# Three convolution steps per attention step on the first chunks, and a looser gate between chunks

## The chip, the cores and the metric

The kernel runs on one core of a Trainium2 chip. The metric is the time of one execution on the device in microseconds, as the median of several runs. The engines named below are TensorE (PE, with its weight loads PEld), VectorE (DVE), ScalarE (ACT), GpSimd (POOL) and SyncE (SP), which here does nothing but issue DMAs.

## The reference, cut to what matters

```python
def _qz_ring(phi):
    c = jnp.cos(phi)
    P = jnp.cumprod(c, axis=-1)
    z0 = jnp.prod(c[..., 1:], axis=-1, keepdims=True)
    return jnp.concatenate([z0, P[..., 1:]], axis=-1)
...
# x: [4, 128, 64, 64]
# layer 0
x = x + _L0_conv_ref(_gn(x), w_off, b_off, w_mask, b_mask, weight, bias)   # deformable 3x3
# layer 1, tokens: [4, 4096, 128], 16 heads of 8
t = _to_tokens(x)
...
qkv = _qz_ring(heads + rx_theta)          # heads come from _ln_t(t); q = k = v
scores = jnp.einsum('bhsd,bhtd->bhst', q, q) / np.sqrt(D)
ctx = jnp.einsum('bhst,bhtd->bhsd', jax.nn.softmax(scores, axis=-1), q)
...
# then w_comb, a norm, a small feed-forward part, a norm;
# at the end a mixture of 8 experts of which each token takes 2
```

The deformable convolution samples the normed image at nine shifted places for each position (four corners each, weighted bilinearly and by a mask), and multiplies the nine samples of 128 channels by a 128 x 128 matrix each. Its result, added to the input, is the residual stream; the attention's queries, keys and values are all the same "features", products of cosines of the normed tokens.

## The kernel before, in words

**Tiles and stages.** An image has 4096 positions, cut into 8 chunks of 512; the 16 heads are 4 groups of 4. A chunk of an image goes through three stages before attention can use it.

1. *Samples* (`deform`). A unit is 128 positions x 3 taps. POOL gathers the corners from a table in DRAM (L622, three indirect DMAs a unit), DVE multiplies by the weights (L642) and adds the four corners (L647, L648). For chunks 0 and 1 of the first image PE transposes the samples (L659) and DVE copies them into `sT_first` (L662). For all other chunks DVE transposes blocks (L685), SP writes them to DRAM (`smd`, L697) and reads them back as `sT` (L730).
2. *Convolution* (`convolved`). 9 taps x 2 halves, each a group of four matmuls that the helper `by_columns` issues (L275), into one PSUM bank `conv_ps`; these 18 groups are what is called "the convolution of a chunk" below. Then DVE adds bias and input (L757), PE transposes (L764), and DVE copies the result to `x2` (L766).
3. *Features* (`features`). Norm statistics (L779, L780), the root on POOL (L390), the normed tokens `xt` (L787), cosines (L367 to L383), products (L815 to L821, into `rn`), a copy by POOL for the values (L822, written by SP at L826), four PE transposes (L835, `fT_ps`), and a high and a low part on DVE (`hiT` L837, `loT` L838), which SP writes as keys and queries with eight DMAs (L845, L846).

**Attention** is a list of *runs*; a run is one group of heads, one chunk of queries (`sc`) and a list of steps of 128 keys. A step has four score matmuls (L1249), two exponentials on ACT (L1258) and four context matmuls into the bank `acc` (L1266). The keys and values of a chunk are loaded at L1227 and L1229, the queries of a run at L1237. Because the first image's features appear chunk by chunk, its first 26 runs (the "opening") work on what there is: runs 0 to 3 take chunk 0 alone (four steps each), runs 4 to 11 add chunk 1 (48 steps), runs 12 to 17 chunk 2 (40 steps), runs 18 to 25 chunk 3. Where a run continues an earlier sum, its partial sum `cu` is loaded from DRAM (L1438), added to `acc` by DVE (L1470), and stored again (L1125); a first sum is copied (L1468).

**Order.** The order of PE, DVE, SP and POOL is fixed at build time by a planner, the class `Beside`. It keeps an estimated clock (`now`, one step is 1.82 us) and estimated times at which DVE and POOL come free. Side work is written as generators, which yield what they need (PE time, DVE time, a wait) before each piece. On every attention step `step` (L132) runs, in this order: up to eight pieces without PE work, one piece with PE work (a "fill", such as one convolution group), and again up to eight pieces without. A fill also needs credit, which a step gives and a fill uses up; the credit may be overdrawn by `LATE`. When attention can't go on, `force` runs side work at once. Emits put into `later` (DMAs of SP, gathers of POOL) go out when the estimated clock gets there. ACT's instructions are the exponentials in the order of the steps.

**The gates.** The list `featuring` holds an entry from the moment a chunk's convolution is queued until its features are done (`featuring.clear()`, L851). The convolution of chunk 0 or 1 is queued only when the list is empty (L672), and so is that of every other chunk (L708). `summed` gets an entry for each finished convolution.

Of the kernel before, what the change touches and what calls it, by code (L numbers as in the profile page):

```python
# [61 lines left out]
class Beside:  # L62
# [9 lines left out]
    def __init__(self):  # L72
        self.now = self.credit = self.dve = self.pool = self.bank = 0.0
        self.lock = None
        self.rate = self.RATE
        self.queue = []
        self.deferred = []

# [53 lines left out]
    def step(self, backlog):  # L132

        self.now += self.STEP
        self.flush(self.now)
        self.credit = min(self.credit + self.rate, self.RATE)
        for fills, limit in ((False, min(0.8, backlog)), (True, backlog), (False, backlog)):
            for _ in range(1 if fills else 8):
                job = next(
                    (j for j in self.queue  # L140
                     if (j["need"][0] > 0) == fills and self._fits(j, limit)), None
                )
                if job is None or (fills and self.credit - job["need"][0] < -self.LATE):
                    break
                self._run(job)

# [50 lines left out]
def need(pe=0.0, dve=0.0, lat=0.0, hold=False, after=0.0):  # L197

    return pe, dve, lat, hold, after
# [17 lines left out]
def kernel(  # L219
# [376 lines left out]
    def deform(b, tab, idx, wt, rest):  # L596


        units = [
            (ch, kg, j) for ch in range(NCH) for kg in range(3) for j in range(4 * ch, 4 * ch + 4)  # L600
        ]
        ahead = []
        issued = 0

        def early(n):

            return b == 0 and n < 3 * 12

        def gather(last):

            nonlocal issued
            while issued < len(units) and issued <= last + (4 if early(issued) else 2):
                n = issued
                issued += 1
                _, kg, j = units[n]
                if early(n) and n % 5 > 2:
                    v = spare(f"v{b}_{j}_{kg}")[:, : 12 * C].rearrange("p (k q) -> p k q", k=3)
                else:
                    v = work.tile([P, 3, 4 * C], F32, tag="v", name=f"v{b}_{j}_{kg}", bufs=NV)
                for k in range(3):  # L620
                    kk = 3 * kg + k
                    nc.gpsimd.indirect_dma_start(  # L622
                        out=v[:, k, :], out_offset=None, in_=tab,
                        in_offset=bass.IndirectOffsetOnAxis(ap=idx[:, j, kk : kk + 1], axis=0),
                    )
                ahead.append((v, beside.gathered()))

        sent = 0.0
        moved = []
        gather(-1)  # L630
        for n, (ch, kg, j) in enumerate(units):
            progress[b] = 0.1 + 0.9 * n / len(units)
            if b == 0 and n == 36:
                yield need(dve=5.0)
                settle()
            while not ahead:
                yield need(lat=0.5)
            v, landed = ahead.pop(0)
            v4 = v.rearrange("p k (q c) -> p (k q) c", c=C)
            w12 = wt[:, j, 3 * kg : 3 * kg + 3, :].rearrange("p k q -> p (k q)")  # L640
            yield need(dve=ve(1536), after=landed)
            nc.vector.tensor_tensor(v4, v4, w12[:, :, None].to_broadcast([P, 12, C]), ALU.mult)  # L642
            if moved:
                yield need(pe=0.01, dve=ve(384))
                moved.pop()()
            yield need(dve=ve(768) + ve(384))
            nc.vector.tensor_tensor(v[:, :, : 2 * C], v[:, :, : 2 * C], v[:, :, 2 * C :], ALU.add)  # L647
            nc.vector.tensor_tensor(v[:, :, :C], v[:, :, :C], v[:, :, C : 2 * C], ALU.add)  # L648
            if b == 0 and ch < 2:


                if n % 12 == 0:
                    while len(summed) < ch:
                        yield need(lat=0.5)
                    sT = big.tile([P, KK, CH], F32, tag="xs", name=f"sT_first{ch}")
                yield need(pe=tr(3), lat=FREE, hold=True)
                pt = misc(f"sT_ps{j}_{kg}")
                for k in range(3):
                    nc.tensor.transpose(pt[:, P * k : P * (k + 1)], v[:, k, :C], ident)  # L659

                def move(sT=sT, kg=kg, i=j % 4, pt=pt):
                    nc.vector.tensor_copy(  # L662
                        sT[:, 3 * kg : 3 * kg + 3, P * i : P * (i + 1)],
                        pt[:, : 3 * P].rearrange("p (k c) -> p k c", c=P),
                    )

                moved.append(move)
                beside.later(beside.now + 0.8, lambda n=n: gather(n))
                if n % 12 == 11:
                    yield need(pe=0.01, dve=ve(384))  # L670
                    moved.pop()()
                    while featuring:  # L672
                        yield need(lat=0.5)
                    featuring.append(True)
                    beside.add("prepare", convolved(b, ch, sT), 0.5, True)
                    if ch == 0:
                        yield from rest
                continue

            yield need(dve=ve(384))  # L680
            if j % 4 == 0:
                beside.flush(sent)
                tr9 = work.tile([P, 4, 4, 4, 32], F32, tag="st", name=f"tr{b}_{ch}_{kg}", bufs=NST)
            for k in range(3):
                nc.vector.transpose(  # L685
                    out=tr9[:, k, :, j % 4, :],
                    in_=v[:, k, :C].rearrange("p (c i) -> p c i", i=32),
                )
            beside.later(beside.dve, lambda n=n: gather(n))
            if j % 4 < 3:  # L690
                continue
            while kg == 0 and len(featuring) > 1:
                yield need(lat=1.0)

            def put(ch=ch, kg=kg, tr9=tr9):
                for o in range(4):
                    nc.sync.dma_start(  # L697
                        out=smd[ch % 2][:, 3 * kg : 3 * kg + 3, :, o].rearrange(
                            "i k c n -> i (k c) n"
                        ),  # L700
                        in_=tr9[32 * o : 32 * (o + 1), :3].rearrange("p k c j t -> p (k c) (j t)"),
                    )

            sent = beside.dve
            beside.later(sent, put)
            if kg == 2:

                while featuring:  # L708
                    yield need(lat=1.0)
                featuring.append(True)  # L710
                beside.later(
                    beside.dve + 0.1,
                    lambda ch=ch: beside.add("prepare", convolved(b, ch), 0.5, True),
                )
        while featuring:
            yield need(lat=1.0)
# [75 lines left out]
    def features(b, ch, x2, mean, rstd):  # L792
# [55 lines left out]
        beside.later(beside.dve - ve(512), lambda: put(0, hi))  # L848
        beside.later(beside.dve, lambda: put(1, lo))
        prepared[b, ch] = beside.dve + 9.0  # L850
        featuring.clear()  # L851

    def prepare(b):
        xs = big.tile([P, KK, CH], F32, tag="xs", name=f"xc{b}")
# [279 lines left out]
    def turn(es, run, t):  # L1134
        b, g, sc = runs[run][:3]
        kt = t % 4
        st = work.tile([P, 4, 4, P], F32, tag="st", name=f"st{run}_{t}", bufs=NST)
        beside.dve = max(beside.dve, beside.now + 0.9)
        for pr in range(2):
            nc.vector.transpose(  # L1140
                out=st[:, :, 2 * pr : 2 * pr + 2, :].rearrange("p o h (q j) -> p o (h q) j", j=32),
                in_=es[pr].rearrange("p h (q o i) -> p o (h q) i", o=4, i=32),
            )
            beside.dve += ve(1024)

        turned = etd[g][sc % 2][kt].rearrange("(o i) r x -> r i o x", i=32)

        def put():
            for r in range(4):
                nc.sync.dma_start(  # L1150
                    out=turned[r], in_=st[32 * r : 32 * (r + 1)].rearrange("p o h x -> p o (h x)")
                )
            turning.discard((g, sc % 2, kt))

        turning.add((g, sc % 2, kt))
        beside.later(beside.dve, put)
# [237 lines left out]
    with tc.manual_schedule(engines={PE, DVE, SP, POOL}):  # L1394
# [6 lines left out]
        while n < len(steps):  # L1401
# [15 lines left out]
            for m in (n, n + 1):  # L1417
                if m < issued and steps[m] in gives:
                    gives.remove(steps[m])
                    turn(es[m - n], *steps[m])  # L1420
            if streaming:
                backlog = 1.5
            else:
                backlog = 0.4 if at >= len(ts) - 3 else 3.2
# [125 lines left out]
```

## Time and profile before

| | |
|---|---|
| five runs, us | 7711.37, 7739.1, 7725.41, 7725.62, 7700.86 |
| median | 7725.41 |
| profiled execution, its own time | 7713.76 |
| its span | 7712.0 |
| busy PE / weight load | 7163.4 (93%) / 2524.6 (33%) |
| busy ACT | 6871.0 (89%) |
| busy DVE | 4480.8 (58%) |
| busy POOL | 1654.6 (21%) |
| exponentials, L1258 | 7400 of 1066 ns, 6867.8 in all |
| context matmuls, L1266 | 29600 of 605 ns, 3963.0 in all |
| score matmuls, L1249 | 14800 of 500 ns (those with a record), 2387.4 in all |

All times are microseconds from the start of the span unless marked ns. Busy times of different engines overlap, so they don't add up to the span. The profile of the first 520 us, in which the first image's opening runs, is where the diff acts: chunk 1 is used first by run 4, chunk 2 by run 12 and chunk 3 by run 18. The first scores of these runs start at 296.04, 405.55 and 492.08; ACT's first exponential of run 4 starts at 296.93 after 71.27 idle, and that of run 12 at 406.15. The features of these chunks reach their transposes (L835) at 264.56, 371.23 and 471.49.

### The profile page before, as it was taken

Reading aid. Unit: us, or ns where it says so; the run is one execution under the profiler, and the core shown is the slowest. Engines: PE = TensorE matmul, PEld = TensorE weight load, DVE = VectorE, ACT = ScalarE, POOL = GpSimd, SP = SyncE. Lnnn points to the kernel's source line nnn. Section 1 sums busy time; section 2 is a strip of 40 time slices with the busy share of each in tenths; the row PEclk is TensorE's granted clock in tenths of the full one; section 3 lists DMA queues with packets and bytes.
Section 4 is the critical chain, followed back from the end, with each engine's and each line's share of the span. In section 5 each row is a group of like instructions: output and inputs, shape, how many; then the busy total and the mean of one; then the engine's idle time right before and its main releaser. Section 6 shows DMA issues by size and latency. Waiting matters only on the chain.

```text
span 7712.0 us, 181988 instructions
## 1 busy us (share of the span) xinstructions
PE 7163.4 (93%) x73736; PEld 2524.6 (33%) x73736; DVE 4480.8 (58%) x8976; ACT 6871.0 (89%) x7441; POOL 1654.6 (21%) x1326
## 2 busy tenths in 40 slices
PE   3589899899999999999999989989999999999997
PEld 2122233223333333333333323333333333333333
DVE  6766356666444767776544676765444545445444
ACT  0579899789999899999999988989999999999995
POOL 5545034443001323422000333431000000000000
PEclk6789999999999999999999999999999999999998
DMA  5677477878557878887766788898665577777762
GB/s 183 204 227 228 131 234 244 285 239 280 161 159 218 264 234 268 277 270 240 209 176 189 240 255 280 286 304 246 188 185 160 151 252 242 246 237 253 240 217 74
DMA packets 922615, 1730.71 MB, mean 224 GB/s; under 512 B 169074, under 2 KB 393356, under 8 KB 871084
## 3 DMA queue, kind: packets, MB, share of 16 engines
q1 hardware_dynamic: 821918, 1412.48, 60.1%
q0 software_dynamic: 92160, 302.06, 12.0%
q8 instruction: 579, 9.49, 0.5%
q10 hardware_dynamic: 7694, 4.52, 0.2%
q14 instruction: 264, 2.16, 0.1%
HBM read 1059.11 MB, written 659.57 MB: 223 GB/s over the span
## 4 chain that ended last, share of the span: by engine, by line
PE 84%; DMA 5%; DVE 4%; issue 3%; ACT 3%; SPq 1%; another core or an unknown queue 0%; POOL 0%; ACTq 0%; POOLq 0%; DVEq 0%
PE acc L1266 41%; PE sc L1249 24%; PE acc L1202 6%; PE conv_ps L275 4%; PE e_ps L275 4%; ACT e L1258 3%; PE f_ps L275 2%; DMA et<-etd 1%; PE om_ps L530 1%; DMA sT<-smd 1%; DMA etd<-st 1%; DVE v L642 1%; PE ao_ps L275 0%; DMA kT<-kTd 0%; DMA qT<-qTd 0%
## 5 line engine op out<-in xcount | busy, mean ns | idle before, releaser
L1258 ACT ACTIVATE e<-sc 128x1024 f32<-128x1024 f32 x7400 | 6867.8, 1066 | 704.4 <-PE sc L1249 425.0
L1266 PE MATMUL acc<-e,qf 128*32 128x512 f32 x29600 | 3963.0, 605 | 23.5 <-DVE cu L1468 13.3
L1249 PE MATMUL sc<-qT,kT 32*128 32x512 f32 x14800 | 2387.4, 500 | 238.6 <-ACT e L1258 142.7
L1249 PEld LDWEIGHTS sc<-qT,kT 32*128 32x128 f32 x14800 | 954.6, 183 | 3635.9 <-ACT e L1258 3055.1
L622 POOL DMA_INDIRECT v<-tab,idx x1152 | 1452.2, 1261 | 1742.3 <-DVE tr L685 1104.6
L1140 DVE STREAM_TRANSPOSE st<-e 128x1024 f32<-128x1024 f32 x792 | 937.6, 1222 | 781.1 <-ACT e L1258 599.6
L1266 PEld LDWEIGHTS acc<-e,qf 128*32 128x32 f32 x29600 | 802.9, 110 | 591.2 <-issue 339.6
L390 POOL TENSOR_TENSOR r<-ln_t,expo 128x4 f32<-128x4 f32 x96 | 112.3, 1170 | 3134.7 <-DVE ln_t L388 3087.5
L642 DVE TENSOR_TENSOR v<-v,wt 128x1536 f32<-128x1536 f32 x384 | 665.9, 1734 | 90.7 <-DMA v<-tab,idx 76.1
L1202 PE MATMUL acc<-et,qf 128*32 128x128 f32 x12672 | 522.3, 281 | 39.5 <-DMA et<-etd 33.4
L1064 DVE TENSOR_TENSOR eo<-e_ps,gt 128x512 f32<-128x512 f32 x256 | 175.1, 686 | 544.4 <-PE e_ps L275 536.8
L1202 PEld LDWEIGHTS acc<-et,qf 128*32 128x32 f32 x12672 | 302.5, 110 | 239.6 <-issue 190.2
L647 DVE TENSOR_TENSOR v<-v 128x768 f32<-128x768 f32 x384 | 367.5, 957 | 9.7
L275 PE MATMUL conv_ps<-sT,wconv_sb 128*32 128x256 f32 x4320 | 352.1, 398 | 16.5 <-DMA sT<-smd 13.8
L1468 DVE COPY cu<-acc 128x512 f32<-128x512 f32 x128 | 88.5, 691 | 385.0 <-PE acc L1266 327.6
L685 DVE STREAM_TRANSPOSE tr<-v 128x128 f32<-128x128 f32 x1080 | 249.4, 282 | 43.6 <-DMA etd<-st 35.1
L648 DVE TENSOR_TENSOR v<-v 128x384 f32<-128x384 f32 x384 | 215.7, 562 | 13.3
L275 PE MATMUL f_ps<-w_sb,h 128*32 128x128 f32 x4096 | 166.5, 281 | 1.3 <-issue 1.2
L390 POOL TENSOR_TENSOR rstd<-lt_t,expo 128x4 f32<-128x4 f32 x32 | 55.7, 1742 | 513.5 <-DVE lt_t L388 504.6
L949 DVE TENSOR_SCALAR h<-h_ps,b_sb 128x512 f32<-128x512 f32 x128 | 94.9, 744 | 102.3 <-PE h_ps L947 91.5
L822 POOL COPY fx<-rn 128x512 f32<-128x512 f32 x32 | 29.6, 925 | 530.3 <-DVE rn L821 348.0
L964 DVE TENSOR_TENSOR a<-a,f_ps 128x512 f32<-128x512 f32 x32 | 22.0, 687 | 199.8 <-PE f_ps L275 199.8
(224 smaller groups left out, 3147.9 us busy)
## 6 DMA issues: line engine op xcount, KB each, us to landing
etd<-st SPq DMA_DIRECT2D x1584, 256.0 KB
et<-etd SPq DMA_DIRECT2D x396, 1024.0 KB
kT<-kTd SPq DMA_DIRECT2D x400, 256.0 KB
smd<-tr SPq DMA_DIRECT2D x360, 192.0 KB
sT<-smd SPq DMA_DIRECT2D x360, 192.0 KB
qf<-fqd SPq DMA_DIRECT2D x400, 144.0 KB
qT<-qTd SPq DMA_DIRECT2D x166, 256.0 KB
atd<-cu SPq DMA_DIRECT2D x128, 256.0 KB
```

Of the source, the lines that this page charges most:

```text
L275: nc.tensor.matmul(dst[c : c + 32], lhsT=lhsT[:, c : c + 32], rhs=rhs, start=start, stop=stop)
L622: nc.gpsimd.indirect_dma_start(out=v[:, k, :], out_offset=None, in_=tab, in_offset=bass.IndirectOffsetOnAxis(ap=idx[:, j, kk : kk + 1], ax ...
L642: nc.vector.tensor_tensor(v4, v4, w12[:, :, None].to_broadcast([P, 12, C]), ALU.mult)
L647: nc.vector.tensor_tensor(v[:, :, : 2 * C], v[:, :, : 2 * C], v[:, :, 2 * C :], ALU.add)
L648: nc.vector.tensor_tensor(v[:, :, :C], v[:, :, :C], v[:, :, C : 2 * C], ALU.add)
L685: nc.vector.transpose(out=tr9[:, k, :, j % 4, :], in_=v[:, k, :C].rearrange("p (c i) -> p c i", i=32),)
L1064: nc.vector.tensor_tensor(ws[hf], pe.rearrange("p (e c) -> p e c", c=C), gt[:, i, 4 * hf : 4 * (hf + 1), None].to_broadcast([P, 4, C]), AL ...
L1140: nc.vector.transpose(out=st[:, :, 2 * pr : 2 * pr + 2, :].rearrange("p o h (q j) -> p o (h q) j", j=32), in_=es[pr].rearrange("p h (q o i ...
L1202: nc.tensor.matmul(acc[32 * h : 32 * (h + 1), P * kt : P * (kt + 1)], lhsT=qf[:, t, QW * h : QW * h + 32], rhs=e[:, :, h, 32 * t : 32 * (t ...
L1249: nc.tensor.matmul(ps[i // 2][:, i % 2, :], lhsT=kT[h : h + 32, P * (t % 4) : P * (t % 4 + 1)], rhs=qT[h : h + 32, :], start=True, stop=True,)
L1258: nc.scalar.activation(e, ps[pr], AF.Exp, scale=1.0 / math.sqrt(HD))
L1266: nc.tensor.matmul(acc[32 * h : 32 * (h + 1), :], lhsT=qf[:, t % 4, QW * h : QW * h + 32], rhs=es[h // 2][:, h % 2, :], start=(t == ts[0]) ...
```

## The change

The diff has two parts.

*Fills.* The planner gets an attribute `fills`, 1 at first. Where it is above 1, `step` runs up to that many pieces with PE work in one step, and the test on the credit is dropped. The main loop sets it to 3 in runs 0 to 11 and to 1 from run 12 on; before the first attention step it has its first value.

*Gates.* The convolution of chunk 0 or 1 is queued without looking at `featuring`. That of a later chunk of the first image waits until the convolutions of all chunks in front are finished (`len(summed) < ch`), and no longer until their features are; the later images keep their gate. At the end of a chunk's features one entry of the list is taken out rather than all.

The line numbers of the changed kernel are one higher than those of the kernel before from L76 on, three higher from L143, one higher from L674, and three higher again from L1421.

```diff
@@ class Beside, __init__
         self.rate = self.RATE
+        self.fills = 1
         self.queue = []
@@ step
         for fills, limit in ((False, min(0.8, backlog)), (True, backlog), (False, backlog)):
-            for _ in range(1 if fills else 8):
+            for _ in range(self.fills if fills else 8):
                 job = next(
                     (j for j in self.queue
                      if (j["need"][0] > 0) == fills and self._fits(j, limit)), None
                 )
-                if job is None or (fills and self.credit - job["need"][0] < -self.LATE):
+                if job is None or (
+                    fills and self.fills == 1 and self.credit - job["need"][0] < -self.LATE
+                ):
                     break
                 self._run(job)
@@ deform, chunks 0 and 1 of the first image
                     moved.pop()()
-                    while featuring:
-                        yield need(lat=0.5)
                     featuring.append(True)
@@ deform, the other chunks
             if kg == 2:
-                while featuring:
+                while len(summed) < ch if b == 0 else featuring:
                     yield need(lat=1.0)
                 featuring.append(True)
@@ features, at the end
         prepared[b, ch] = beside.dve + 9.0
-        featuring.clear()
+        featuring.pop(0)
@@ the main loop, before step is called
                     turn(es[m - n], *steps[m])
+
+            beside.fills = 3 if run < 12 else 1
             if streaming:
```

## The prediction

> **What bounds the kernel now.** I read the page first: ScalarE (ACT) is busy for 89% of the span, TensorE (PE) for 93%, nearly all of it in the attention steps (L1249 scores, L1258 exponential, L1266 context). Its slices show both low only in the first tenth. Then the table by stage of that tenth:
>
> ```profile
> 175.00:226.00 51.00, 38.85 (x301) 13.21 (x305) 34.17 (x47) 30.57 (x32) 41.09 (x32) 0.77 0.73 234
> 226.00:296.00 70.00, 5.52 (x61) 3.30 (x53) 62.73 (x130) 0.00 (x0) 42.50 (x31) 0.55 0.65 196
> 296.00:400.00 104.00, 93.17 (x700) 27.84 (x700) 63.05 (x120) 86.09 (x93) 43.84 (x32) 0.90 0.70 211
> 400.00:520.00 120.00, 96.84 (x748) 28.29 (x744) 75.76 (x137) 88.92 (x96) 58.52 (x45) 0.84 0.80 238
> ```
>
> Columns: stretch, length, busy time (and count) of PE, weight load, DVE, ACT, POOL, then granted clock, DMA share, GB/s. From 226 to 296 ACT does nothing and PE 5.5 of 70 us, while DVE works 62.7 of 70: attention has used up chunk 0 and waits for chunk 1's features. From 296 to 520 DVE is busy 139 of 224 us, so there it has some 85 us to spare. PE's timeline shows the chain inside the hole:
>
> ```profile
> 198.75 1.08 PE L275 MATMUL conv_ps<-sT_first,wconv_sb 128*32 128x256 f32 x8
> ...
> 226.20 3.14 PE L275 MATMUL conv_ps<-sT_first,wconv_sb 128*32 128x256 f32 x44
> 238.79 1.09 PE L764 MATMUL x_ps<-ident,xr 128*128 128x128 f32 x4 [9.45 <-issue]
> 264.56 1.09 PE L835 MATMUL fT_ps<-ident,rn 128*128 128x128 f32 x4 [24.68 <-DVE rn L821]
> 296.04 1.22 PE L1249 MATMUL sc<-qT,kT 32*128 32x512 f32 x6 [30.39 <-DMA kT<-kTd]
> ```
>
> Chunk 1's convolution is spread over 31 us of attention; its result then queues on DVE behind products of chunk 2 (residual add at 237.57), and after the features SP's queue makes the last gap:
>
> ```profile
> 269.31 0.66 SPq L845 DMA_DIRECT2D kTd<-hiT  x1
> ...
> 277.20 6.15 SPq L697 DMA_DIRECT2D smd<-tr  x4
> 283.40 1.10 SPq L721 DMA_DIRECT2D xr<-in_x_dram  x1
> 284.59 2.79 SPq L730 DMA_DIRECT2D sT<-smd  x4
> 287.43 0.43 SPq L1227 DMA_DIRECT2D kT<-kTd  x1
> ```
>
> The keys' load waits 10 us behind chunk 2's smd, xr and sT issues.
>
> **The change, edit by edit.** The order of instructions on each engine, the two kernels side by side, says what the planner makes of it. *The gates* (L672, L708, L851): with these alone the order on every engine is that of before, so they cost and bring 0; no cover is needed, since nothing moves. *Three fills a step*: chunk 1's 72 matmuls go out in six bursts of 12 instead of fours, the first one step earlier; chunk 2's mostly in twelves too; DVE, SP and POOL follow. ACT's order is the same throughout, no instruction is added or removed, and after chunk 6's features all orders are equal again, so whatever is won or lost by then stays. I follow the chain by rows.
>
> 1. *PE.* A step of before with one group is 0.44 (L1249) + 0.57 (L275) + 0.86 (L1266) = 1.87 us in the chain of waits; ACT alone needs 0.92 x 2 = 1.84 (34.97 us for 38). With a burst it is 0.44 + 3 x 0.57 + 0.86 = 3.0: each burst holds ACT up by 1.16 us, some 12 bursts 14 us, behind no cover. The convolution ends at 196.87 + 3.05 (first burst, cold) + 5 x 1.7 + 4 x 0.87 + 4 x 0.44 = 213.7 instead of 229.3.
> 2. *DVE.* The residual add now stands behind cu1 and the tenth block's multiply: 214.3, x2's copy 218.2 (before 242.44). Then copy and statistics 2.7, cu2 0.7, v11 3.3, xt 1.1, cosine and products 12.2, cu3 0.7: rn ends at 238.9 (before 264.4). rstd on POOL (2.5 us) hides behind v11, as its gather queue is empty by 218. A stream transpose and one multiply (2.35) stand before hiT: 241.2, loT to 242.6 (before 269.2). The eight blocks of chunk 2 (28 to 35) that stood ahead, 8 x 3.95 = 31.6 us (1.72 + 0.96 + 0.56 + 0.70), are done later, under ACT's work of runs 4 to 7. Chunk 2's gathers now queue on POOL behind fx (239 to 241); five units x 3.9 us from 241 still keep ahead of DVE, which ends chunk 2 at 272 (before 273.8).
> 3. *SP.* One smd group 2.7, fqd 2.65, eight key and query writes 7.8, to 252.9; the load may go when they have landed, 4.15 us in chunk 0 (164.87 to 169.02), so 257.1. From load to first score it took 5.5 us in chunk 0 and 8.6 in chunk 1: 262.6 to 265.7, and I take 264. Run 4 starts 32 us earlier than 296.04. smd, xr and sT of chunk 2 now come behind the keys, where they have until 286.
> 4. *Runs 4 to 11.* qT5 goes out at 265 behind the next smd and lands in 7.1 as before (301.89): 272, against 309.1. Eight steps at 1.84, six with bursts at 3.0, 21 at 1.84: 344. There cu10's partial sum waits behind chunk 2's key writes on SP (issued 347, landing in 4 to 8.5): 351 to 356. Run 12's exponential follows 12.2 (without the 3.44 us wait for kT) to 15.6 us later: 367, against 406.15. Gain 39.
> 5. *Runs 12 to 18.* 40 steps took 83.4 us (406.15 to 489.5); kept, they end at 450.4. Here the change adds a wait: chunk 3's transposes (L835), which stood 12 steps ahead of that end (471.49), now stand behind the last context matmul. On PE run 18's scores queue behind them; hiT, the eight writes, smd 3.8, xr 0.9, four loads 1.8 and eight sT issues 6.7 then put qT19 at 474, and with the 11.3 us that it took (504.81 to 516.09) run 19 starts at 485.3, against 516.1. Gain 31: eight of the 39 are given back.
> 6. *After.* Same matmuls, nearly the same order; the stall of run 34 (863 to 906) hangs on chunk 7's order, which is equal. 0, with -8 to +8 for the waits between 568 and 604 and from 692 to 700, which can fall either way.
>
> **Rules against the rows.** The first group took 1.08 us where the granted clock was low and 0.64 later; if all six bursts ran at the first, they would end at 196.9 + 6 x 3.24 + 4 x 1.93 + 4 x 0.8 = 227, and the gain would fall by 13.6. [...]
>
> qT19 took 11.3 us in a stretch (484 to 517) with a DMA share of 0.94, against 5.5 for chunk 0's first keys; by the short one the gain is 37, and I take the long one, as the same transfers bunch. [...]
>
> **The sum.** 7713.76 us is the profiled execution (span 7712.0, 1.8 around it); minus 31 is 7683. It lies 11.7 below the median of the five runs (7725.41); against the median that is **7694**.
>
> **Rivals.** *More is kept* (10%): qT19 comes in 5.5 us and the waits at 568 and 692 shrink by 8: 7725 - 45 = 7680. For it: those waits sit in DMA-crowded stretches that come apart. Against: SP's order there is nearly the same. *Given back* (23%): the gain of 32 us at run 4 is real but run 18's new wait and the bursts eat it: cold bursts take 13.6, late features of chunk 3 some 6 more: 31 - 20 = 11, 7714. For it: L835 now has nothing behind which to hide. Against: DVE has 85 us to spare before it. *DVE debt* (7%), the other side: the 31.6 us of blocks moved behind chunk 1's features make chunks 2 and 3 late by as much, so run 19 keeps its date (gain 0), while the bursts' 14 and the exposed 8 stay: 7725 + 22 = 7747. It decides once DVE has no idle time between 296 and 517; the table gives it 85 us. *That it does nothing* holds for the gates; for the fills PE's order rules it out.
>
> **Chances.** My sum, 60%, with its own range of 22 to 42 us of gain, 7683 to 7703. A measurement of this kernel tells some 0.3%, 23 us, from no change. Of the 60, 56 lie beyond that, with the 10 above: 0.66 faster; 4 and the 23: 0.27 same; 0.07 slower. The range takes in the first rival and most of the second: 7668 to 7726.
>
> **What would show it.** In the changed kernel's profile: six rows of L278 with some 24 records between 197 and 214; the residual add (L758) near 214; first scores of run 4 at 262 to 266 and the hole in ACT down from 71 to some 37 us; conv 2 in bursts from some 287; run 12 near 367; L836 of chunk 3 only after run 17's last L1267 and a hole of some 20 us there; run 19 near 485. I am wrong if DVE is busy without a break from 296 to 450, if bursts stay at 1.08 a group, or if the lead at run 12 is not near 39 us.

## The result: 7 us, where 31 were forecast

The changed kernel takes 7721.62 us (median of 24 runs, 7707.44 to 7738.11), the kernel before 7729.03 (44 runs): ratio 0.9993, 95% interval 0.9986 to 1.0000. It is at most a hair faster, well inside the 0.3% that the prediction called no change. Chips differ by more: the kernel before took 7591 to 7760 us on those used below, so only ratios on one chip are compared. Two executions, one of begin40 (13058 us) and one of the kernel before beside deep3 (19932 us), ran at granted clocks of 0.46 and 0.58 where all others had 0.96 to 0.97, and no ratio takes them in.

The changed kernel's table by stage shows the hole filled and opened again later. Columns as in the prediction: stretch, length, busy time and count of PE, weight load, DVE, ACT, POOL, granted clock, DMA share, GB/s.

```profile
175.00:226.00 51.00, 39.95 (x320) 13.94 (x324) 30.34 (x53) 27.05 (x29) 32.42 (x28) 0.78 0.64 211
226.00:296.00 70.00, 29.57 (x168) 8.20 (x160) 64.68 (x121) 24.59 (x27) 42.72 (x30) 0.66 0.78 238
296.00:400.00 104.00, 85.55 (x668) 26.54 (x668) 64.74 (x121) 81.64 (x88) 47.59 (x38) 0.91 0.75 225
400.00:520.00 120.00, 83.88 (x660) 26.10 (x652) 77.99 (x143) 70.03 (x76) 59.08 (x45) 0.80 0.74 219
```

From 226 to 296 ACT now works 24.6 us where it did nothing; from 296 to 520 it works 151.7 instead of 175.0. DVE does the same work as before in each row, within 4 us. ACT's exponentials come in the same order in both kernels, so the first one of each run can be set side by side in the two traces (us):

| first exponential of run | 4 | 6 | 7 | 12 | 14 | 18 | 19 | 26 | 34 | 39 | 46 |
|---|---|---|---|---|---|---|---|---|---|---|---|
| before | 296.93 | 326.70 | 333.99 | 406.15 | 422.71 | 492.97 | 516.98 | 630.00 | 816.48 | 915.64 | 1198.16 |
| changed | 267.10 | 297.29 | 310.50 | 383.42 | 406.30 | 499.42 | 518.88 | 628.14 | 811.50 | 911.32 | 1199.33 |
| difference | -29.8 | -29.4 | -23.5 | -22.7 | -16.4 | +6.5 | +1.9 | -1.9 | -5.0 | -4.3 | +1.2 |

Thirty microseconds are won at run 4, and all are gone at run 18. The later differences, up to 16 us either way after run 50, are those of single executions.

PE's timeline of the changed kernel (start, duration, operation, count, idle time before and what ended it) shows the win and the loss:

```profile
196.04 2.79 PE L278 MATMUL conv_ps<-sT_first,wconv_sb 128*32 128x256 f32 x24
...
199.48 2.05 PE L278 MATMUL conv_ps<-sT_first,wconv_sb 128*32 128x256 f32 x24
...
202.76 1.50 PE L278 MATMUL conv_ps<-sT_first,wconv_sb 128*32 128x256 f32 x24
...
242.81 1.12 PE L836 MATMUL fT_ps<-ident,rn 128*128 128x128 f32 x4 [12.16 <-DVE rn L822]
266.21 1.22 PE L1250 MATMUL sc<-qT,kT 32*128 32x512 f32 x6 [22.28 <-issue]
...
468.17 3.37 PE L1267 MATMUL acc<-e,qf 128*32 128x512 f32 x24
471.48 0.66 PE L836 MATMUL fT_ps<-ident,rn 128*128 128x128 f32 x4
498.53 1.22 PE L1250 MATMUL sc<-qT,kT 32*128 32x512 f32 x6 [26.40 <-DMA kT<-kTd]
```

Chunk 1's convolution goes out in bursts of three groups, its features reach the transposes at 242.81 instead of 264.56, and run 4 follows. Chunk 3's features reach theirs at 471.48, directly behind run 17's last context matmuls. Before, that was at 471.49, with nine steps of attention still to come; that the two dates agree so closely is chance. Attention arrives 17 us earlier (run 17's last exponential ends at 470.4, before at 487.1) and waits. The chunk that it waits for has not moved at all, so the lead turns into a wait for the keys: 26.40 us, where run 18's first scores had 2.62 before:

```profile
492.08 1.22 PE L1249 MATMUL sc<-qT,kT 32*128 32x512 f32 x6 [2.62 <-issue]
```

SP's timeline of the changed kernel (start, duration, line, operation, count) shows the keys of chunk 1, which now go ahead of the last `smd` and of `xr` and `sT`, and then those of chunk 3:

```profile
250.00 1.08 SPq L846 DMA_DIRECT2D kTd<-hiT  x1
...
257.32 0.93 SPq L847 DMA_DIRECT2D qTd<-loT  x1
262.80 0.34 SPq L1228 DMA_DIRECT2D kT<-kTd  x1
...
266.90 4.13 SPq L698 DMA_DIRECT2D smd<-tr  x4
...
474.86 0.55 SPq L846 DMA_DIRECT2D kTd<-hiT  x1
...
482.22 0.69 SPq L847 DMA_DIRECT2D qTd<-loT  x1
486.67 3.83 SPq L698 DMA_DIRECT2D smd<-tr  x4
...
491.21 1.21 SPq L1228 DMA_DIRECT2D kT<-kTd  x1
```

Chunk 1's load goes 4.6 us after the last key write's issue ends. Chunk 3's goes 8.3 after it, behind a `smd` of chunk 4. SP stood idle in front of that `smd` for 3.7 us, until DVE had done chunk 4's last sample, whose gather had come late:

```profile
482.57 1.76 DVE L645 TENSOR_TENSOR v<-v,wt 128x1536 f32<-128x1536 f32 x1 [5.41 <-DMA v<-tab,idx]
```

So a few us of the 26.4 are SP's order and chunk 4's sample; the rest is the date of the features.

That chunk 3 did not move is seen in each of its steps, from the same traces:

| chunk 3 | first and last multiply (L642) | last four sT issues, from | convolution | transposes of its features |
|---|---|---|---|---|
| before | 278.6, 379.2 | 413.4 | 412.3 to 447.0 | 471.49 |
| changed | 284.9, 377.2 | 411.0 | 410.4 to 442.6 | 471.48 |

What held it there is mostly PE's order. Counted in steps of attention (eight records of context matmuls each), its convolution stands behind 72 steps now and stood behind 65 before, and its transposes stand behind 104 and stood behind 95. Seven and nine steps of 1.84 us are 13 and 17 us; attention's lead is 16 to 17 us from run 14 on. In front of the convolution PE has no idle time, now or before, so there the convolution waited for the attention steps ahead of it and not for its samples:

```profile
410.41 0.64 PE L278 MATMUL conv_ps<-sT,wconv_sb 128*32 128x256 f32 x8
```

```profile
412.31 0.64 PE L275 MATMUL conv_ps<-sT,wconv_sb 128*32 128x256 f32 x8
```

The planner sets these places by its own estimate of when the samples are there, so samples can act through the order as well as by themselves.

### The profile page after: what moved, and what is told of

Read it like the earlier page. It is cut to its first block, busy times and chain, and to the rows that moved or that the text cites. A ratio compares the mean times of both kernels' runs of the same rounds, so it can differ in the third digit from the quotient of the medians.

```text
span 7726.7 us, 181999 instructions
## 1 busy us (share of the span) xinstructions
PE 7181.7 (93%) x73736; PEld 2528.5 (33%) x73736; DVE 4481.5 (58%) x8976; ACT 6870.9 (89%) x7441; POOL 1647.3 (21%) x1326
## 4 chain that ended last, share of the span: by engine, by line
PE 82%; DMA 6%; DVE 4%; ACT 3%; SPq 2%; issue 2%; another core or an unknown queue 0%; POOL 0%; ACTq 0%; DVEq 0%; POOLq 0%
PE acc L1267 40%; PE sc L1250 24%; PE acc L1203 5%; PE conv_ps L278 4%; PE e_ps L278 4%; ACT e L1259 3%; PE f_ps L278 2%; DMA et<-etd 1%; DMA sT<-smd 1%; PE om_ps L533 1%; DMA etd<-st 1%; DMA qT<-qTd 1%; DVE v L645 1%; PE ao_ps L278 0%
## 5 line engine op out<-in xcount | busy, mean ns | idle before, releaser
L1267 PE MATMUL acc<-e,qf 128*32 128x512 f32 x29600 | 3971.6, 606 | 32.6 <-DVE cu L1473 18.6
L1065 DVE TENSOR_TENSOR eo<-e_ps,gt 128x512 f32<-128x512 f32 x256 | 175.0, 685 | 549.2 <-PE e_ps L278 539.1
L651 DVE TENSOR_TENSOR v<-v 128x384 f32<-128x384 f32 x384 | 215.8, 562 | 13.3
```

The source lines that it names most:

```text
L1065: nc.vector.tensor_tensor(ws[hf], pe.rearrange("p (e c) -> p e c", c=C), gt[:, i, 4 * hf : 4 * (hf + 1), None].to_broadcast([P, 4, C]), AL ...
L1267: nc.tensor.matmul(acc[32 * h : 32 * (h + 1), :], lhsT=qf[:, t % 4, QW * h : QW * h + 32], rhs=es[h // 2][:, h % 2, :], start=(t == ts[0]) ...
```

## The experiments

Three theories at first. P: the dates at which a chunk's samples are taken (gathers on POOL, products on DVE) set when later runs may start. G: the gain is given back at one place, run 18's key writes. B: the bursts hold ACT up. D, a rival of P later on: DVE's work alone sets the samples' dates. All the kernels compute the same result as before.

For every kernel, the table gives the difference of a run's first exponential from that in gates_only, which has the order of before (negative is earlier; us), and the measured ratio to the kernel before on the same chip with its interval. The kernels in it ran on chips where before took 7591 to 7595 us. Each difference is of two single executions: begin40 and changed_again, which have the same order up to run 38, differ by up to 3 us there (6 once), and so much means nothing.

| kernel | run 4 | 12 | 18 | 26 | 31 | 38 | 39 | 46 | ratio to before |
|---|---|---|---|---|---|---|---|---|---|
| changed_again | -32.1 | -22.1 | +1.2 | -5.3 | -7.1 | -7.1 | -9.0 | -6.1 | 0.9990 (0.9981 to 1.0000) |
| begin40 | -32.5 | -22.0 | +2.3 | -3.3 | -4.3 | -4.4 | -24.3 | -37.3 | 0.9995 (0.9985 to 1.0005) |
| fills4 | -34.3 | +0.3 | -9.9 | -5.5 | -6.3 | -4.2 | -22.5 | -35.5 | 1.0000 (0.9990 to 1.0010) |
| fills18 | -32.7 | -21.2 | -16.6 | -22.9 | -0.2 | +0.8 | +3.5 | -9.6 | 1.0035 (1.0020 to 1.0049) |
| deep3 | -32.2 | -22.2 | -21.2 | -23.6 | -22.5 | -22.6 | -24.3 | -26.4 | 0.9974 (0.9964 to 0.9984) |
| deep3_again | -33.3 | -22.7 | -23.3 | -23.3 | -22.3 | -22.4 | -23.6 | -24.5 | 0.9959 (0.9946 to 0.9972) |
| before_deep3 | +3.9 | +12.8 | +15.1 | +14.7 | +10.0 | +9.8 | -13.1 | -16.3 | 1.0009 (0.9999 to 1.0019) |
| deep8 | -32.9 | -20.8 | +6.7 | +13.8 | +25.8 | +24.8 | -1.4 | -13.7 | 1.0035 (1.0022 to 1.0047) |
| before_deep8 | +2.7 | +14.3 | +20.4 | +17.4 | +28.4 | +28.3 | +2.2 | -10.4 | 1.0031 (1.0020 to 1.0043) |
| deep3_borders | -23.0 | -15.8 | -15.3 | -15.9 | -18.5 | -18.6 | -31.7 | -36.1 | 0.9965 (0.9952 to 0.9978) |
| deep3_fills18 | -33.7 | -22.3 | -28.4 | -37.0 | -21.6 | -19.6 | -26.6 | -39.6 | 0.9981 (0.9972 to 0.9990) |

**gates_only: one fill throughout.**

```diff
-            beside.fills = 3 if run < 12 else 1
+            beside.fills = 1
```

> The change with one fill a step throughout; the looser gates stay. Theory P (samples set the pace: the dates at which the samples of chunks 3 to 7 are taken decide when runs 18 to 39 start), theory G (the gain of 30 us at run 4 is given back at one place, run 18, because chunk 3's transposes and key writes have nothing left to hide behind) and theory B (the bursts hold ScalarE up) all expect the kernel before: same order on every engine, 7729 within 6, run 4's first exponential near 297 and run 39's near 915.

Ratio 1.0003 (0.9993 to 1.0012); run 4 at 292.25, run 39 at 902.81 (this chip is a faster one: before took 7591 us on it, not 7729). The gates do nothing by themselves; no run has the fills without them.

**begin40: a control.**

```diff
-                if not beside.has("prepare") and b + 1 < NB and ...
+                if run >= 40 and not beside.has("prepare") and b + 1 < NB and ...
```

> The changed kernel, with the preparation of the second image begun not before run 40 instead of run 38. A control for the next kernels, which need the same edit: all theories expect the changed kernel's time, 7722 within 6, with the same dates up to run 38 (run 4 near 267, run 18 near 499, run 34 near 811).

As expected up to run 38 and in its time. Between 38 and 39 it gains 20 us, because the second image's first loads and border writes no longer stand on SP ahead of chunk 7's keys, which the second half of run 38 needs and run 39 follows (their load goes 2.4 us after the last key write's issue, in gates_only 18.9); the gain is 37 at run 46 and gone at the end. fills18, fills4, deep8, before_deep8 and deep3_fills18 have this edit too.

**fills18: bursts for chunk 3 too.**

```diff
-            beside.fills = 3 if run < 12 else 1
+            beside.fills = 3 if run < 18 else 1
```

> begin40 with three fills a step up to run 17 instead of run 11, so that chunk 3's convolution goes out in bursts too. G: the loss at run 18 is local; chunk 3's features come some 20 us earlier, run 18 starts near 478, and what is won there stays: 20 us less than begin40, about 7702. P: run 18 starts near 478 as well, but the samples of chunks 4 to 7 come no earlier, so the lead melts by run 39, whose first exponential comes as late as in begin40 within 6 us, and the time is begin40's within 8. B: six more bursts, 6 us longer than begin40.

This run decides between G and P. Run 18 starts at 475.3, as both expected. PE's timeline has the wait for chunk 3 shrunk from begin40's 24.73 us:

```profile
474.43 1.22 PE L1250 MATMUL sc<-qT,kT 32*128 32x512 f32 x6 [3.97 <-issue]
```

Chunk 3's samples were no earlier for that (last multiply 374.0, in begin40 373.1), and its transposes still came at 449.85 instead of 467.90. So with the same samples chunk 3 can be 18 us earlier: up to run 18 it was the spread of its convolution over attention's steps in PE's order that held it up.

But the lead of 14 to 27 us over begin40 that runs 18 to 26 have is gone at run 31. It goes in two waits for queries, in front of runs 27 and 31, which begin40 doesn't have at these places:

```profile
626.94 0.80 PE L1250 MATMUL sc<-qT,kT 32*128 32x512 f32 x4 [11.43 <-DMA qT<-qTd]
728.24 0.80 PE L1250 MATMUL sc<-qT,kT 32*128 32x512 f32 x4 [10.31 <-DMA qT<-qTd]
```

On SP these loads go out at 615.40 and 717.30, behind the `smd`, `xr` and `sT` issues of chunks 5 and 6 (from 596.13 and from 704.91): the chunks' traffic has not come earlier (chunk 5's last multiply is at 587.3, in begin40 at 581.3), and attention, being early, runs into it. Then the last chunk decides, as P said, and worse: chunk 7's last multiply is at 800.5 against begin40's 773.0, its last key write at 890.4 against 861.4, and run 39 starts 16 to 17 us behind that write in both (906.3 and 878.6). The time is 28 us above begin40's, as much as the difference of 27.7 at run 46 (the two profiled executions end 42 apart). A lead at run 18 does not stay by itself: G falls. P's forecast of the time, within 8 us of begin40's, was missed too.

**fills4: bursts for chunk 1 alone.**

```diff
-            beside.fills = 3 if run < 12 else 1
+            beside.fills = 3 if run < 4 else 1
```

> begin40 with three fills a step up to run 3 alone: chunk 1's convolution in bursts, chunk 2's in fours. B: the six bursts of run 6 and 7 go, 6 us are won there and kept: 7716. G: run 12 is some 20 us later than in begin40 (near 404), run 18 waits as before, the time is some 8 us longer than begin40 at most. P: run 12 near 404, but run 18 near 499 and run 39 as in begin40 within 6 us; time as begin40 within 8.

Run 12 is back at 402.4, where gates_only has it (402.1): the whole lead of 22 us at run 12 hangs on chunk 2's bursts. Run 18 starts 12 us earlier than in begin40, which I had not expected. Chunk 3's convolution stands behind 64 steps there, not 72, and starts at 392.55 (407.13), after 28 us in which PE waited for its samples, and its transposes come at 459.68 (467.90). But the two kernels meet by run 38 (-4.2 and -4.4), and the time is 5 us longer, inside the interval. B's six us were not won.

**deep3 and before_deep3: five gather buffers for chunk 3.**

```diff
         def early(n):
-            return b == 0 and n < 3 * 12
+            return b == 0 and n < 4 * 12
```

> The changed kernel with five gather buffers instead of three for the samples of chunk 3 as well (four units of gathers ahead instead of two, in buffers that stand idle then). Theory P (samples set the pace, and their pace is set by the few gathers that may be in flight): chunk 3's last multiply comes about 14 us earlier than in the changed kernel (which has 377), run 18 about 12 earlier (near 485), and as the samples of chunks 4 to 7 follow, run 39 too is some 12 earlier (near 899 of 911) and the time 12 us shorter: ratio to before near 0.998. Theory D (VectorE's work sets the dates of the samples, however many gathers are in flight): last multiply of chunk 3 at 377 within 4, run 18 and run 39 as in the changed kernel, ratio near 0.9993. Theory G (the loss sits at run 18's key writes alone): run 18 within 4 of the changed kernel's 499.

> The kernel before, one fill a step, with the same five buffers for chunk 3. P: no burst is needed: run 4 starts as before (near 297), chunk 3's and later samples come 10 to 20 us earlier than before, run 39 some 15 us earlier (near 900 of 915), time 15 us shorter than before: ratio near 0.998. D: samples, run 18, run 39 and time as before, ratio 1.000. G: at most run 18's own wait moves, by under 5 us.

With the bursts the deeper gathers bring what P said and more: chunk 3's last multiply is at 361.5 (begin40 373.1), its transposes at 451.0 (467.9), run 18 at 470.7, and a lead of 16 to 28 us stays to the end. DVE's waits from 260 to 400 (what it waited for, us in all, times, longest), first begin40, then deep3, show what the buffers do:

```profile
DVE v L645 <- DMA v<-tab,idx: 13.8, 3, 7.2
```

```profile
DVE v L645 <- DMA v<-tab,idx: 5.9, 3, 3.4
```

The same products wait 8 us less for their gathers. That is against D: the work is the same, and the dates moved. PE's order moved with them: the convolution stands behind 67 steps instead of 72, the transposes behind 98 instead of 104. So this run does not tell the samples' dates from the order; fills18 moved chunk 3's transposes as far with its samples where they were. In the kernel before, the same edit brings the samples of chunk 3 forward by 34 us (last multiply 340.8, in gates_only 375.2) and wins nothing. Its convolution starts at 394.1, 15 us earlier (gates_only 408.8), but its transposes come at 468.8, no earlier than in gates_only (467.9), and the samples' block writes (`smd`) go out on SP ahead of run 5's queries, as SP's and then PE's timeline show:

```profile
299.99 8.17 SPq L697 DMA_DIRECT2D smd<-tr  x4
308.21 3.31 SPq L1237 DMA_DIRECT2D qT<-qTd  x2
```

```profile
317.37 0.80 PE L1249 MATMUL sc<-qT,kT 32*128 32x512 f32 x4 [9.39 <-DMA qT<-qTd]
```

Runs 5 to 19 are later by 6 to 15 us. P's "no burst is needed" was wrong: bursts without samples win 5 to 8 us, samples without bursts none, and both together 20 to 31.

**deep8 and before_deep8: five buffers for all eight chunks**, with begin40's edit: the same line with `n < 8 * 12`.

> begin40 with five gather buffers for the samples of all eight chunks of the first image. P: the samples of chunks 4 to 7 run ahead of the steps, the waits for chunks 4 to 7 (runs 19 to 39) go, run 34 starts some 8 us and run 39 some 14 us earlier than in begin40, chunk 7's features come over 50 us earlier than its 854; time 14 us less than begin40, ratio to before near 0.9975. D: chunk 7's features within 10 us of begin40's, time as begin40, ratio near 0.9995.

> The kernel before with five gather buffers for all eight chunks, and the second image begun not before run 40 as in begin40. P: chunk 7's features over 40 us earlier than before's 858 to 872, run 39 without a wait for them, some 30 us earlier than before; the time within 8 us of deep8's, as what the bursts win in the opening is not needed. D: chunk 7's features within 10 us of before, time as before within 6.

Half of P held: chunk 7's last key part is ready at 793.8, 62 us earlier than in begin40. The other half failed: the time is 1.0035 and 1.0031. PE's timeline of deep8 has a wait in front of run 18 that is longer than deep3's (9.95), and new ones in front of runs 23 and 27:

```profile
497.69 0.80 PE L1250 MATMUL sc<-qT,kT 32*128 32x512 f32 x4 [18.17 <-DMA kT<-kTd]
...
588.75 0.80 PE L1250 MATMUL sc<-qT,kT 32*128 32x512 f32 x4 [14.38 <-DMA qT<-qTd]
...
663.93 0.80 PE L1250 MATMUL sc<-qT,kT 32*128 32x512 f32 x4 [14.29 <-DMA qT<-qTd]
```

Samples of chunk 4 were taken (last multiply 423.9, in deep3 460.2) at the cost of chunk 3's features: 38 us from x2's copy to the transposes (433.9 to 471.8) instead of 27 (424.3 to 451.0). For 8.77 of these 11 us DVE waits in the middle of the features for a partial sum, whose load stands on SP behind chunk 4's `smd`, `xr` and `sT`. Samples taken too early can cost time too; the piece that attention needs next must come first.

**A second round on one chip: changed_again, deep3_again, and two additions to deep3.** deep3_fills18 is deep3 with `3 if run < 18` and begin40's edit; deep3_borders moves the border writes of the second image:

```diff
-        if b == 1:
-            borders(tab, nc.sync)
...
+        if b == 0:
+            borders(tabs[1], nc.scalar)
```

> The changed kernel itself, beside the next three on one chip. All theories: ratio to before 0.9993 within 0.001, run 18 within 4 us of before's 492, run 39 some 4 us ahead of before's 903.

> deep3 once more, with more rounds. Theory P (the lead that the bursts win stays only as far as the samples of the later chunks follow; with five buffers for chunk 3 they follow): ratio 0.9974 within 0.001, run 18 some 20 us ahead of before and run 38 too. If deep3's 20 us were an accident of its one set of runs: 0.9993.

> deep3, with the border writes of the second image's corner table issued by ScalarE's queue before attention begins, instead of SyncE's queue ahead of run 39's key load (13 us of issues there in deep3). If SyncE's queue is what is left of run 39's wait: run 39 starts 13 us earlier than in deep3 (near 865 of 878), run 38 unchanged, and the time falls by 13 us, ratio near 0.9957. If a lead won there is lost again later, as begin40 lost its 20 us between run 46 and the end: ratio as deep3's, 0.9974.

> deep3 with three fills a step up to run 17 and the second image begun not before run 40. Theory G (a lead at run 18 stays): run 18 some 10 us ahead of deep3's 471, kept to the end, ratio near 0.996. P: run 18 some 10 us ahead, but the samples of chunks 4 to 7 come no earlier than deep3's, the further lead is gone by run 38, and the time is deep3's or longer, ratio 0.9974 or above; run 39 about 16 us behind chunk 7's last key write.

The change (0.9990) and deep3's gain (0.9959) repeat, the latter a little larger than expected; on this chip deep3_again is 22 us below changed_again. deep3_fills18 has run 18 at 463.4, 7 us ahead of deep3, and 13 ahead at run 26; by run 31 deep3 is in front, and the time is 15 us longer than deep3_again's on the same chip: P again, G not. In deep3_borders attention begins 10 us late (run 0 at 185.31 instead of 175.6), run 39 still comes 7 us earlier than in deep3, and the time can't be told from deep3's.

**deep3_late: the border writes later on SP.**

```diff
-            borders(tab, nc.sync)
+            beside.later(beside.now + 40.0, lambda: borders(tab, nc.sync))
```

> deep3 with the border writes of the second image's corner table put 40 us later on SyncE's queue, behind run 39's key load. If that queue is all that is left of run 39's wait: in deep3 chunk 7's last key write is issued at 843.5 and the key load at 861.7; without the borders the load goes at some 848, and run 39's first exponential comes at 854 to 858 instead of 878.5; 20 us, kept to the end as deep3_borders' 8 were: ratio near 0.994. If run 39 waits for something else, such as chunk 7's writes or their landing: run 39 within 6 us of 878. If the lead is lost later: run 39 near 856 but the time deep3's, ratio 0.9965 to 0.9975.

SP's timeline of deep3 around chunk 7's keys, and then that of deep3_late:

```profile
844.85 2.40 SPq L858 DMA_DIRECT2D xc<-in_x_dram  x4
...
847.99 6.18 SPq L323 DMA_DIRECT2D tab<-zero  x1
...
854.90 5.62 SPq L323 DMA_DIRECT2D tab<-zero  x1
...
861.71 0.46 SPq L1228 DMA_DIRECT2D kT<-kTd  x1
```

```profile
869.72 2.66 SPq L858 DMA_DIRECT2D xc<-in_x_dram  x4
...
873.78 0.43 SPq L1228 DMA_DIRECT2D kT<-kTd  x1
```

The key load goes 5 us after the last key write's issue instead of 18. Chunk 7's first scores then come 13.6 us after that write's end instead of 24.4 (882.65 and 868.46 on PE): 11 us, not 20. The 20 took the date of these scores for that of run 39's first exponential, which four steps of run 38 still precede (10 us). And of the 13 us that the load gained, some 2 went to the second image's norm, for which PE now waits in front of the scores:

```profile
882.13 0.59 PE L454 MATMUL gn_pm<-gn_mv,gm 128*128 128x1 f32 x2 [9.38 <-DVE gn_mv L451]
```

deep3 has this wait too (7.91 at 855.83), ahead of a longer one for the keys. So the queue was one part of run 39's wait, and with it gone the next one in line shows. The ratio, 0.9956 (0.9939 to 0.9972; 7728.57 against 7759.91 on a slower chip), is below the kernel before and the change, but can't be told from deep3's.

## Why the prediction was wrong, point by point

**What bounds the kernel** was read rightly as far as run 4: ACT idle, DVE in the chain, chunk 1's features.

**The gates** bring nothing, as said (1.0003). **PE's bursts** had the right size. The convolution ended at 215.6 (213.7 forecast). Chunk 2's six bursts lengthen the stretch from run 6 to run 7 by 5.9 us (13.2 against 7.3), 1.0 each (1.16 forecast). Chunk 1's took 2.79, 2.05 and then 1.50 us each: the granted clock was 0.50 from 196.0 to 199.5, 0.82 to 202.7 and 1.00 after that. Two bursts were slow, not one and not six, and the 13.6 us of cold bursts did not come. The sum has a first burst alone at the low clock (3.05 us, and 1.7 for each of the five behind it); no run shows that. In the changed kernel PE's work resumed at 194.50, after 4.11 us idle, and the granted clock was 0.50 up to 200.5 and 1.00 from 201.0, so it rose 6.0 to 6.5 us after that, inside the second burst.

**DVE and SP up to run 4** were right within 6 us at each row: residual add 217.2 (214.3), rn's end 242.8 (238.9), keys' load 262.8 (257.1). First scores came at 266.2, 2 us behind the forecast; the load took 3.4 us from issue to scores, and not the 5.5 to 8.6 of the rows that I used.

**Runs 4 to 11** (gain 39 at run 12; measured 22.7) were the first failure. I let chunk 2's convolution begin at some 287 and had cu10 issued at 347. It began at 297.05, mostly because the eight blocks of chunk 2 that went behind chunk 1's features ended its samples later, not earlier (its end was at 279.5, before at 273.8; I had 272). What chunk 2 gained it gained from the bursts alone: 20 us of convolution instead of 39. fills4 shows it: without them there is no lead at run 12 (+0.3). So its key writes still stood in front of cu10's load on SP:

```profile
349.78 3.38 SPq L698 DMA_DIRECT2D smd<-tr  x4
353.26 1.07 SPq L846 DMA_DIRECT2D kTd<-hiT  x1
...
363.44 1.18 SPq L1441 DMA_DIRECT2D cu<-part  x1
```

DVE's add of cu10 came at 370.40, and not at 351 to 356. I had named this very queue, with a date 14 to 19 us too early. "The lead at run 12 is not near 39 us" was one of my three signs of being wrong, and the only one that came.

**Runs 12 to 18** is the step that failed most. The order was read rightly: the transposes "now stand behind the last context matmul" (472 on PE, no idle time between), where they had stood 9 steps ahead of it (not 12), and the hole that I had put at some 20 us came, with 26.4. Two terms were wrong. "40 steps took 83.4 us; kept, they end at 450.4": they ended at 471.5, 21 us later. Of these, 16 came with run 12's date, and 5 from the steps themselves, which took 88.1 us with waits for a partial sum (5.21, at 399.38) and for queries (1.50, at 405.41). And the way from there to qT19's issue took 33.2 us (471.5 to 504.7), where I had 23.6: my list has no time for SP's wait for chunk 4's last sample, nor for the issues in that crowded stretch taking longer than before (eight of `sT` 7.6 us, not 6.7). Of this exposed way I had counted 8 us as lost; it was 20.

I also took chunk 3's features as ready whenever attention came there. Their products (rn) were finished at 470.7, at the same moment as attention, since both run on behind chunk 3's convolution in PE's order; nothing shows that they would have been ready at 450. fills18 and deep3 show two ways to have them earlier: the convolution in bursts, or its samples, and with them its place in the order, earlier.

For qT19 the long price was the right one: 13.3 us from issue (504.73) to run 19's first scores (518.03) in a stretch (484 to 518) with a DMA share of 1.02, where I took 11.3. That the transfers bunch there was my estimate; no run here isolates what made this one long.

In numbers, the lead forecast for run 19 was 31 us and the measured one -1.9: 33 short, of which 2 were lost by run 4, 14 from there to run 12, 5 by the end of run 17, 10 on the way to qT19's issue beyond the 8 that I had counted, and 2 in qT19's load.

**After run 18**, "whatever is won or lost by then stays" was wrong as a rule, though it cost little here (from +1.9 to -5.0 at run 34). fills18 loses all of its 14 to 27 us after run 18, first to the traffic of chunks 5 and 6 and then to chunk 7's date, which run 38's second half waits for in every kernel but those of deep8.

**The rivals.** *Given back* came nearest in size (7714), and half for the right reason: L835's new place did expose the way to run 19, at 20 us and not 14, while the cold bursts did not come. *More is kept* failed at once: qT19's load took the long price. *DVE debt* named the right outcome, run 19 keeping its date, but not its size (chunk 2's samples ended 6 us later, not 31.6, and chunk 3's 2 us earlier), and with a test that could not find it. I looked at DVE's busy time, and it does idle 81 us from 296 to 520, 85 before. That idle time was no reserve: products wait for gathers (15.3 us from 264 to 500) and partial sums for PE in a fixed order. I should have asked for the date of chunk 3's last sample in the new order, where that sample's convolution stands on PE, and what paces one unit: some 9 us before and 8 now (100.6 and 92.3 us from the first of 12 products to the last), where its DVE work is 3.95.

What stays open: how much of deep3's gain is the samples' dates and how much the order that the planner makes from them; where begin40 and its kin lose, after run 46, the 20 us that they gain at run 39; and why chunk 3's samples are 11 us earlier in fills4 than in begin40 (last multiply 362.0 and 373.1). No run was made for any of these.

## What to carry to other kernels

A stage that is sped up keeps its gain only if the stages behind it are fed as early; follow the chain to the next wait on each resource that feeds it (here samples, convolution, features, keys, chunk by chunk), and compare absolute dates beside positions in the order. Idle time of an engine whose order is fixed, such as DVE's 81 us here, is not capacity: ask what each idle stretch waits for, and how many transfers may be in flight. Where two small edits each win almost nothing, try them together: bursts alone won 5 to 8 us (with intervals that reach to none), buffers alone none, both 20 to 31.

## What the hardware showed that I had not expected

The same program took 7591, 7592, 7595, 7729 and 7760 us (medians) on the chips of this study, 2.2% apart. Its granted clock was 0.964 to 0.969 in its runs on the fastest of these chips and 0.960 to 0.964 on the slowest, some 0.4% apart in the mean, so most of the difference is not in that clock. And a load's time from issue to first use was 3.4 us for run 4's keys and 7.4 for run 5's queries (256 KB each) in the same stretch of the changed kernel; one price for these two does not fit.
